# Neighbour sums of layer 0: one PSUM bank per block of rows, or two

## The chip, the cores and the metric

The kernel runs on one core of a Trainium2 chip. The metric is the device time of one execution in microseconds (us). The engines meant below are TensorE (PE, with its weight loads shown apart as PEld), VectorE (DVE), ScalarE (ACT), GpSimd (POOL) and SyncE (SP, which here only issues transfers). Each engine runs its own list of instructions strictly in the order in which the kernel issued them, and waits for others by semaphores.

## The reference, cut to what matters

Two graph layers over 4096 nodes with 512 features and a 4096 x 4096 0/1 matrix `adj`. Layer 0 is the one that is changed:

```python
Ab = A > 0
keep = Ab & (jnp.cumsum(Ab.astype(jnp.int32), axis=1) <= neibor_num)   # the first 64 neighbours
cnt = keep.sum(axis=1, keepdims=True).astype(X.dtype)
nb_sum = keep.astype(X.dtype) @ X
nb_mean = nb_sum / jnp.maximum(cnt, 1.0)
xj = jax.nn.leaky_relu(nb_mean @ W_nb.T + b_nb)
xi = jax.nn.leaky_relu(X @ W_line.T + b_line)
return xi + jnp.where(cnt > 0, xj, jnp.zeros((), X.dtype))
```

The layer's output is `x1 = layernorm(x + that)`. Layer 1 is a graph attention over all neighbours of `adj` (scores, softmax, a product with `x1 @ W`), again with a residual and a layernorm.

## The kernel before, in words

The 4096 rows are 32 blocks of 128 rows (`NB`, `P`). The kernel never forms `nb_mean @ W_nb.T`: it first computes `y = x @ W_nb.T` and then sums rows of `y`, so that the neighbour sum is `keep @ y`. `y` is kept in SBUF as two rounded parts, `y_hi` and `y_lo` (type fp32r, a float32 that PE takes in one pass), whose sum is `y` to float32's precision. The last six blocks of `y` lie in tiles named `hi` and `lo`.

Before the neighbour sums, the products with `W_nb` and `W_line` run (`seven`, L554; their matmuls are those of L512). From there on, beside the matmuls, the rows of `adj` are turned into codes in 64 steps, two for each block of rows (`NCH` is 2). One step is: SP loads a piece of `adj` (`load_adj`, L154), ACT makes flags of it (`edge`, L167), DVE scans it for the first 64 neighbours (`scan_sums` and `scan_codes`, L181 and L197: five instructions of L189, L190, L194, L201, L202), and ACT packs the outcome into bytes which POOL's queue stores to memory (`pack`, L215). After every fourth step DVE also derives the neighbour counts (`count`, L206). Thirteen of the 64 steps are done when the neighbour sums begin, and the rest are spread over them at 58/32 steps a block (`RATE`, L672): mostly two a block, sometimes one.

The neighbour sums (the loop at L725) go over 128 groups `s`, four to a block of rows `i`. A group is 8 x 128 neighbours. Its mask `kt` is made by ACT from the codes (`make_kt`, L268; the codes come back turned by a transposing transfer on SP, `load_kt`, L675). Each 128 x 128 piece of the mask is the stationary operand of two matmuls of 512 columns, one for `y_hi` and one for `y_lo`, and all 64 matmuls of a block add up in one PSUM bank, `accs[i]`. So a block is 64 matmuls and the stage 2048.

What is put in the engines' lists around this, in the order of the code, for group `s` = 4i + g:

- ACT: `make_kt(s + 2)`. It writes over the mask of group s - 1 (three buffers), so it waits for that group's matmuls. At g = 2 the activation of the block before follows, `bend0(i - 1)` (L691, instruction at L693), and then the ACT parts of a code step (`codes_late`, L248).
- SP: the transposed load for block i + 2 at g = 0, a load of `x` for block i at g = 2, and the load of `adj` for the code step two ahead.
- PE: the 16 matmuls.
- DVE: `finish(i - 1, g)` (L695), the ending of the block before. At g = 0 the sum is scaled by `rcnt` (one over the count) and the bias is added, reading the PSUM bank (L700). At g = 2 it is multiplied by `some` (count above 0), added to the rest (L706), and the layernorm's statistics follow (L118, L123, L125; the power of -1/2 is POOL's, L127). At g = 3 the layernorm is applied (L132) and the row block stored. At g = 0 of the next block two sums of products (L718) close it. `codes_step` (L254) then adds DVE's part of a code step.

So in ACT's list the activation of block i - 1, which waits for DVE's L700, stands ahead of the masks of later groups, and in DVE's list the endings and the code steps stand in one line.

PSUM has 8 banks: `ps_s` holds two (`pt`), `ps_acc` six (`acc`), which are handed out in turn. Blocks 0 and 1 take the two `pt` banks, since the `acc` banks are still in use by the stage before; block 2 and all later ones take an `acc` each. Behind the stage layer 1 takes `acc` banks from the same ring (L1217), while `finish(31, ...)` (L1152), the counts (L1159 to L1163) and their stores (L1171) stand ahead of ACT's copies of the first products (L1225).

The order within one engine is the order of the calls in the program; there is no scheduler in between.

Of the kernel before, what the change touches and what calls it, by code (L numbers as in the profile page):

```python
# [9 lines left out]
F32 = mybir.dt.float32  # L10
# [5 lines left out]
ALU = mybir.AluOpType  # L16
# [4 lines left out]
P = 128  # L21
# [11 lines left out]
def two_layer_adj_gnn(  # L33
# [16 lines left out]
    nc = tc.nc  # L50
    N, C = x.shape
    NB = N // P
    NC = C // P
# [19 lines left out]
    ps_s = ctx.enter_context(tc.tile_pool(name="ps_s", bufs=2, space=PSUM))  # L73
    ps_acc = ctx.enter_context(tc.tile_pool(name="ps_acc", bufs=6, space=PSUM))
# [12 lines left out]
    rcnt = const.tile([P, NB], F32, name="rcnt")  # L87
# [14 lines left out]
    def x1_blk(b):  # L102

        n, k = divmod(b // 2, 4)
        return x1_d[k].rearrange("(n q r) c -> n r q c", n=4, r=2)[n, b % 2]
# [4 lines left out]
    wa_rows, bias_nb = late[0:2], late[2]  # L110
# [5 lines left out]
    def ln_stats(y):  # L116
        st = stat.tile([P, nc.vector.BN_STATS_DIM], F32, name="st")
        nc.vector.bn_stats(st, y)  # L118
        return ln_rs(st)
# [10 lines left out]
    def ln_apply(y, stats):  # L130
        mv, rs = stats
        nc.vector.tensor_scalar(y, y, mv[:, 0:1], rs, ALU.subtract, ALU.mult)  # L132
# [5 lines left out]
    with ExitStack() as l0:  # L138
# [7 lines left out]
        y_hi, y_lo = ({i: t[:, i, :] for i in range(EDGE)} for t in y_most)  # L146
# [101 lines left out]
        def codes_late(n=1):  # L248

            for part, q in late_q[:n]:  # L250
                part(q)
            del late_q[:n]

        def codes_step(s):  # L254
            while done[0] < min(s, NB * NCH + 1):
                codes_late(2)
                q = done[0]
                load_adj(q + 2)
                scan(q)
                late_q.extend([(edge, q + 1), (pack_late, q - 1)])  # L260
                done[0] += 1

        KB = 8
        NS = NB // KB
        ktbs, kts, accs, owns, fin = {}, {}, {}, {}, {}
        y_again = []

        def make_kt(s):  # L268
            if s < NB * NS:
                b, g = divmod(s, NS)  # L270
                if s not in kts:
                    kts[s] = ktb_p.tile([P, KB // 2, 2, P], F32R, name="kt")
                bytes_ = ktbs[b].bitcast(U8)[:, ts(g, KB // 2), :]
                nc.scalar.activation(  # L274
                    kts[s], bytes_.rearrange("p t (i r) -> p t r i", r=2),
                    AF.Sigmoid, bias=steep[:, 1:2], scale=STEEP,
                )


        with ExitStack() as la:  # L280
# [40 lines left out]
            def early(name):  # L321
                t = adj_p.tile([P, CH], BF16, name=name).bitcast(F32)
                return t.rearrange("p (c q) -> p c q", q=C)

            raw = {}
            for name, form in (("nb", "p (c q) -> p c q"), ("line", "p (j q) -> p j q")):
                t = adj_p.tile([P, CH], I32, name="a").bitcast(F32)
# [3 lines left out]
            for k in range(2):  # L331
                t = early("left")
# [3 lines left out]
            t = early("edge")  # L336
# [336 lines left out]
        start = done[0]  # L673

        def load_kt(b):  # L675
            if b < NB:
                if packed[0] < NCH * (b + 1):
                    codes_late(2)
                assert done[0] > NCH * (b + 1)
                ktbs[b] = ktb_p.tile([P, NT, P], BF16, name="ktb")  # L680
                nc.sync.dma_start_transpose(ktbs[b], code_d[b])
# [3 lines left out]
        def place(name, bufs=2):  # L685

            if spare:
                return spare.pop(0)
            return work.tile([P, C], F32, name=name, bufs=bufs)

        def bend0(i):  # L691
            if i >= 0:
                nc.scalar.activation(fin[i], fin[i], AF.Prelu, alpha=SLOPE)  # L693

        def finish(i, g):  # L695
            if i < 0:
                return
            if g == 0:
                t = place("t")
                nc.vector.scalar_tensor_tensor(  # L700
                    t, accs.pop(i), rcnt[:, i : i + 1], bias_nb, ALU.mult, ALU.add
                )
                fin[i] = t
            elif g == 2:
                t, y = fin[i], owns.pop(i)
                nc.vector.scalar_tensor_tensor(  # L706
                    y, t, some[:, i : i + 1], y, ALU.mult, ALU.add
                )
                fin[i] = y, ln_stats(y)
            elif g == 3:  # L710
                y, stats = fin[i]
                ln_apply(y, stats)
                nc.gpsimd.dma_start(x1_blk(i), y)
            elif g == 4:
                y, _ = fin.pop(i)
                for k in range(2):
                    junk = place("junk", 1)
                    nc.vector.scalar_tensor_tensor(  # L718
                        junk, y, 1.0, wa_rows[k], ALU.mult, ALU.mult,
                        accum_out=e12[:, 1 - k, i : i + 1],  # L720
                    )
# [3 lines left out]
        for s in range(NB * NS):  # L725
            i, g = divmod(s, NS)
            if s == 2:
                for n in range(0, 4, 2):
                    hi, lo = (t[:, n : n + 2, :] for t in y_again)
                    nc.scalar.copy(hi, lo.bitcast(F32))  # L730
                    nc.vector.tensor_tensor(lo, lo.bitcast(F32), hi.bitcast(F32), ALU.subtract)
            make_kt(s + 2)
            if g == 2:
                bend0(i - 1)
            codes_late()
            if g == 0:
                load_kt(i + 2)
                if i < 2:
                    accs[i] = ps_s.tile([P, NC, P], F32, name="pt").rearrange(
                        "p k c -> p (k c)"  # L740
                    )
                else:
                    accs[i] = ps_acc.tile([P, C], F32, name="acc")
            if g == 2:
                if i < NB - 1:
                    owns[i] = place("own")
                    nc.sync.dma_start(owns[i], x_blk(i))
            if g == 3 and i < NB - 1:
                nc.gpsimd.dma_start(owns[i], own_d[i], accum_op=ALU.add)
            kt = kts.pop(s)  # L750
            turns = list(range(KB))
            if s == NS - 1:
                turns = turns[:2] + turns[6:] + turns[2:6]
            for n, k in enumerate(turns):
                j = g * KB + k
                for term in (y_hi, y_lo):
                    nc.tensor.matmul(  # L757
                        accs[i], kt[:, k // 2, k % 2, :], term[j],
                        start=(g == n == 0 and term is y_hi),
                        stop=(g == NS - 1 and n == KB - 1 and term is y_lo),  # L760
                    )
            if g == 0:
                finish(i - 2, 4)
            finish(i - 1, g)
            codes_step(start + int((s + 1) * RATE / NS))
        finish(NB - 2, 4)


# [13 lines left out]
    NS = 32  # L782
# [427 lines left out]
    for j in range(NS):  # L1210
        g, h = divmod(j, 2)
        if g < PLAIN:
# [4 lines left out]
            bank = ps_acc.tile([P, 2, HC], F32, name="acc")  # L1217
            (yrs, xvs)[g].append(bank)
            x1t = x1ts.pop(j)
            for m in range(NC):  # L1220
                nc.tensor.matmul(  # L1221
                    bank.rearrange("p h c -> p (h c)"), x1t[:, m, :], ws[:, m, :],
                    start=(m == 0), stop=(m == NC - 1),
# [23 lines left out]
    for q in range(NP * NT):  # L1247
        g, k = divmod(q, NP)
# [38 lines left out]
    p, rz = banks[NT - 1], rzs[NT - 1]  # L1287
# [64 lines left out]
```

## Time and profile before

| what | value |
|---|---|
| median of 3 runs | 1550.19 us (1549.63 to 1551.04) |
| the profiled execution, its own time | 1549.75 us |
| its span, from the first instruction to the last | 1548.0 us |
| PE busy | 1537.9 us (99% of the span) |
| DVE busy | 1265.5 us (82%) |
| ACT busy | 985.5 us (64%) |
| POOL busy | 269.5 us (17%) |
| the neighbour sums in the chain of waits | 203.85 us to 668.36 us |
| granted TensorE clock | 0.999 of full speed |

Times inside the execution are counted from the span's start. The profiled execution's time is 1.75 us longer than its span, and lies 0.44 us below the median. A row of the profile that groups instructions reads: line, engine, operation, output<-inputs (names without buffer numbers), shape, count, then busy time and mean duration. A row of the timeline reads: start, duration, engine, line, operation, output<-input, and in brackets how long the engine had been idle before and what ended that. Durations of matmuls overlap: the time that one costs is the distance from its start to the next one's. The same is true, by less, on DVE and ACT.

### The profile page before, as it was taken

How to read it: one execution, taken by the hardware profiler on the slowest of the kernel's cores; microseconds unless marked ns; L12 is line 12 of the kernel's file. 1: busy time of each engine (PE TensorE's matmuls, PEld its weight loads, DVE VectorE, ACT ScalarE, POOL GpSimd, SP SyncE). 2: the span in 40 equal slices, each digit the busy share in tenths (PEclk: the TensorE clock that was granted, in tenths of full speed). 3: DMA queues.
4: the chain of work that ended last, by engine and by line, in shares of the span. 5: the costliest groups of instructions: out<-in, count | busy, mean ns of one | idle time of the engine just before them, and what ended most of it. 6: DMA issues, size and time to landing. Idle time of an engine off the chain costs nothing.

```text
span 1548.0 us, 19196 instructions
## 1 busy us (share of the span) xinstructions
PE 1537.9 (99%) x6592; PEld 1241.4 (80%) x6592; DVE 1265.5 (82%) x2349; ACT 985.5 (64%) x1190; POOL 269.5 (17%) x428
## 2 busy tenths in 40 slices
PE   9999999999999999999999999999999999999998
PEld 5444478888888888878888888888888888888887
DVE  6888759999999999378887888888888888888864
ACT  3666678888888887427685567555675556755520
POOL 4445322212222212120001101111011110111101
PEclk9999999999999999999999999999999999999999
DMA  7965598879888887653122212222122221222201
GB/s 196 249 208 185 192 251 265 251 244 256 259 257 256 238 263 193 152 135 104 47 58 55 51 32 69 66 58 51 32 69 67 57 52 33 68 67 57 52 4 55
DMA packets 178434, 203.28 MB, mean 131 GB/s; under 512 B 102224, under 2 KB 138832, under 8 KB 170016
## 3 DMA queue, kind: packets, MB, share of 16 engines
q1 hardware_dynamic: 150080, 131.78, 30.2%
q0 software_dynamic: 26544, 68.69, 16.9%
q10 hardware_dynamic: 1712, 1.59, 0.4%
q8 instruction: 52, 0.85, 0.2%
q14 instruction: 46, 0.38, 0.1%
HBM read 142.08 MB, written 43.13 MB: 120 GB/s over the span
## 4 chain that ended last, share of the span: by engine, by line
PE 98%; DMA 1%; DVE 1%; ACT 0%; ACTq 0%; issue 0%; POOLq 0%; DVEq 0%; SPq 0%
PE acc L1094 36%; PE acc L757 28%; PE pt L1094 14%; PE acc L512 11%; PE acc L908 5%; PE pt L757 2%; PE acc L1221 1%; DMA bias_line<-in_L_gnn_b_line_dram 0%; DMA a<-in_L_gnn_W_nb_dram 0%; DMA c<-in_x_dram 0%; PE acc L373 0%; PE acc L350 0%; DVE t L406 0%; DVE hi L519 0%; DVE hi L534 0%; ACTq L292 0%
## 5 line engine op out<-in xcount | busy, mean ns | idle before, releaser
L1094 PE MATMUL acc<-bt,s 128*128 128x256 f32 x1504 | 335.7, 379 | 0.0
L1094 PEld LDWEIGHTS acc<-bt,s 128*128 128x128 f32 x1504 | 285.8, 190 | 38.9
L757 PE MATMUL acc<-y_hi,kt 128*128 128x512 f32 x780 | 303.4, 389 | 0.0
L757 PE MATMUL acc<-y_lo,kt 128*128 128x512 f32 x780 | 303.4, 389 | 0.0
L979 ACT ACTIVATE w<-nat,few 128x1024 f32<-128x1024 uint8 x128 | 137.0, 1137 | 237.8 <-DVE a L1054 237.8
L1094 PE MATMUL acc<-bt,a 128*128 128x256 f32 x1056 | 239.0, 379 | 0.0
L1094 PE MATMUL pt<-bt,a 128*128 128x256 f32 x992 | 224.5, 379 | 0.0
L1094 PEld LDWEIGHTS acc<-bt,a 128*128 128x128 f32 x1056 | 200.6, 190 | 27.3
L1094 PEld LDWEIGHTS pt<-bt,a 128*128 128x128 f32 x992 | 188.5, 190 | 25.6
L1054 DVE STREAM_TRANSPOSE a<-w 128x1024 f32<-128x1024 f32 x128 | 153.2, 1226 | 61.5 <-ACT w L1035 51.0
L274 ACT ACTIVATE kt<-ktb,few 128x1024 fp32r<-128x1024 uint8 x124 | 142.7, 1152 | 87.4 <-PE acc L757 71.7
L127 POOL TENSOR_TENSOR rs<-ve,few 128x1 f32<-128x1 f32 x64 | 46.8, 731 | 811.0 <-DVE ve L125 791.1
L757 PEld LDWEIGHTS acc<-y_lo,kt 128*128 128x128 f32 x780 | 146.5, 188 | 30.5
L757 PEld LDWEIGHTS acc<-y_hi,kt 128*128 128x128 f32 x780 | 146.3, 188 | 30.4
L972 ACT ACTIVATE w<-w,st_n 128x1024 f32<-128x1024 f32 x128 | 149.3, 1233 | 16.1 <-DVE m L989 16.1
L1035 ACT ACTIVATE w<-w,nm 128x1024 f32<-128x1024 f32 x128 | 145.5, 1138 | 11.1 <-DVE nm L1026 11.1
L989 DVE CUSTOM_DVE_ANT_0 w<-e_n,w 128x1024 f32<-128x1024 f32 x128 | 149.5, 1221 | 1.3
L171 ACT ACTIVATE edge<-a,few 128x2048 bf16<-128x2048 int32 x64 | 136.3, 2130 | 6.0 <-DMA a<-in_adj_dram 6.0
L219 ACT CAST code<-left 128x2048 uint8<-128x2048 bf16 x64 | 121.1, 1892 | 0.0
L202 DVE TENSOR_TENSOR left<-edge,left 128x2048 bf16<-128x2048 bf16 x64 | 78.4, 1225 | 2.2
L190 DVE TENSOR_TENSOR_SCAN left<-few,ends,left 128x1024 bf16<-128x1024 f32 x32 | 75.2, 2351 | 1.1
L512 PE MATMUL acc<-hi,lo 128*128 128x512 f32 x160 | 73.8, 593 | 0.4 <-ACT acc L568 0.4
(236 smaller groups left out, 2048.6 us busy)
## 6 DMA issues: line engine op xcount, KB each, us to landing
a<-in_adj_dram SPq DMA_DIRECT2D x64, 1024.0 KB, 5.7
code_d<-code POOLq DMA_DIRECT2D x64, 256.0 KB, 3.8
nat<-code_d SPq DMA_DIRECT2D x248, 64.0 KB, 2.2
w<-x_d SPq DMA_DIRECT2D x128, 64.0 KB, 2.2
own<-in_x_dram SPq DMA_DIRECT2D x31, 256.0 KB, 3.1
own<-own_d POOLq DMA_DIRECT2D x31, 256.0 KB, 4.6
x_d<-own POOLq DMA_DIRECT2D x31, 256.0 KB, 4.4
out_dram<-c POOLq DMA_DIRECT2D x30, 256.0 KB, 2.8
```

What stands on the lines that cost most here:

```text
L171: nc.scalar.activation(edge_of[s], loaded.pop(s).rearrange("p (t q) -> p q t", q=2), AF.Sigmoid, bias=steep[:, 0:1], scale=STEEP, accum_ou ...
L202: nc.vector.tensor_tensor(left, e, left, ALU.mult)
L219: nc.scalar.copy(code.bitcast(U8).rearrange("p (t q) -> p q t", q=2), seen_of.pop(s))
L274: nc.scalar.activation(kts[s], bytes_.rearrange("p t (i r) -> p t r i", r=2), AF.Sigmoid, bias=steep[:, 1:2], scale=STEEP,)
L512: nc.tensor.matmul(bank, lhs[:, k, :], rhs[:, k, :], start=start and k == 0, stop=k == 1, skip_group_check=True,)
L757: nc.tensor.matmul(accs[i], kt[:, k // 2, k % 2, :], term[j], start=(g == n == 0 and term is y_hi), stop=(g == NS - 1 and n == KB - 1 and ...
L972: nc.scalar.activation(dst, src, AF.Prelu, bias=bias, scale=scale, alpha=0.2)
L979: nc.scalar.activation(wts[b][:, i, :], nats[b, i // 2].bitcast(U8)[:, i % 2, :], AF.Relu, bias=far, scale=-FAR,)
L989: nc.vector.tensor_tensor_reduce(w_i, e2_n, w_i, 1.0, -3e38, ALU.subtract, ALU.max, m4s[b][:, i : i + 1])
L1035: nc.scalar.activation(w_i, w_i, AF.Exp, bias=nms[b][:, i : i + 1], accum_out=z4s[g][:, r, i : i + 1])
L1054: nc.vector.transpose(a[:, r].rearrange("p s (i a) -> p i s a", a=SQ), wts[2 * g + r][:, :, ts(k, 8 * SQ)].rearrange("p i (s x) -> p i s x ...
L1094: nc.tensor.matmul(banks[g][n], lhs[:, j, :], bt[:, 4 * k + j, rhs, :], start=(k == 0 and j == 0 and n == mate[0]), stop=(k == NP - 1 and ...
```

## The change

A block gets two banks instead of one. The matmuls with `y_hi` add up in the first and those with `y_lo` in the second; their order stays: `hi`, `lo`, `hi`, `lo`. The ending at g = 0 then has two DVE instructions of the same kind: the first scales the low sum and adds the bias, the second scales the high sum and adds the first one's output. Block 0 takes both `pt` banks, and all later blocks take `acc` banks in pairs, so that six banks hold three blocks where they held six. Nothing else is edited; DVE has 32 instructions more, and the lists of the other engines keep their instructions and order.

```diff
             if g == 0:
                 t = place("t")
+                of_hi, of_lo = accs.pop(i)
                 nc.vector.scalar_tensor_tensor(
-                    t, accs.pop(i), rcnt[:, i : i + 1], bias_nb, ALU.mult, ALU.add
+                    t, of_lo, rcnt[:, i : i + 1], bias_nb, ALU.mult, ALU.add
+                )
+                nc.vector.scalar_tensor_tensor(
+                    t, of_hi, rcnt[:, i : i + 1], t, ALU.mult, ALU.add
                 )
                 fin[i] = t
...
-                if i < 2:
-                    accs[i] = ps_s.tile([P, NC, P], F32, name="pt").rearrange(
-                        "p k c -> p (k c)"
-                    )
+                if i < 1:
+                    accs[i] = [
+                        ps_s.tile([P, NC, P], F32, name="pt").rearrange("p k c -> p (k c)")
+                        for _ in range(2)
+                    ]
                 else:
-                    accs[i] = ps_acc.tile([P, C], F32, name="acc")
+                    accs[i] = [ps_acc.tile([P, C], F32, name="acc") for _ in range(2)]
...
                 j = g * KB + k
-                for term in (y_hi, y_lo):
+                for bank, term in zip(accs[i], (y_hi, y_lo)):
                     nc.tensor.matmul(
-                        accs[i], kt[:, k // 2, k % 2, :], term[j],
-                        start=(g == n == 0 and term is y_hi),
-                        stop=(g == NS - 1 and n == KB - 1 and term is y_lo),
+                        bank, kt[:, k // 2, k % 2, :], term[j],
+                        start=(g == n == 0), stop=(g == NS - 1 and n == KB - 1),
                     )
```

In the changed file L700 becomes L701, the added instruction is L704, L706 becomes L710 and the matmuls' L757 becomes L762.

## The prediction

> **What bounds the kernel now.** I read the chain of waits first. PE carries 98% of it. In order of time, the stage that the change touches is one unbroken piece of PE work:
>
> ```profile
> PE 98%; DMA 1%; DVE 1%; ACT 0%; ACTq 0%; issue 0%; POOLq 0%; DVEq 0%; SPq 0%
> ...
> 203.85 29.31 PE pt L757 x128
> 233.16 435.20 PE acc L757 x1920
> 668.36 10.30 PE acc L1221 x24
> ...
> 770.46 8.63 PE acc L1094 x40
> ```
>
> (start, length, work). 435.20 us over 1920 matmuls is 226.7 ns each: 3.63 us a group of 16, 14.51 us a block. Nothing holds PE in this stage, so the question is what the other engines have to spare. The busy time by stretch, while code steps still run and after them:
>
> ```profile
> 233.00:610.00 377.00, 377.00 (x1665) 312.18 (x1664) 350.02 (x556) 315.70 (x270) 88.20 (x125) 1.00 0.86 252
> 610.00:668.36 58.36, 58.36 (x259) 48.34 (x258) 28.93 (x60) 24.23 (x23) 10.24 (x17) 1.00 0.54 128
> ```
>
> (length, then PE, PEld, DVE, ACT, POOL busy, PE's clock, DMA share, GB/s). DVE is busy 350.02 of 377 us, and the rest is hardly free time. Its waits there are:
>
> ```profile
> DVE own L132 <- POOL rs L127: 11.0, 15, 0.8
> DVE left L189 <- ACT code L219: 3.2, 3, 1.2
> DVE own L706 <- ACT t L693: 2.1, 3, 0.7
> ```
>
> The 11.0 us are a latency behind DVE's own L125: they come wherever L132 follows it directly, however late DVE is. Only 3.2 + 2.1 = 5.3 us are waits of a DVE that is early; the other 10.7 us are the steps between 556 instructions. DVE is all but full until about 618 us, where the last code step ends; behind that it is half idle.
>
> How late DVE already runs, and what stands behind it, the timelines of PE, DVE and ACT show at the start of block 21 (first matmul at 508.62):
>
> ```profile
> 508.40 0.39 PE L757 MATMUL acc<-lo,kt 128*128 128x512 f32 x1
> 508.62 0.39 PE L757 MATMUL acc<-y_hi,kt 128*128 128x512 f32 x1
> 508.85 0.39 PE L757 MATMUL acc<-y_lo,kt 128*128 128x512 f32 x1
> ```
>
> ```profile
> 516.98 0.75 DVE L700 SCALAR_TENSOR_TENSOR t<-acc,rcnt,c 128x512 f32<-128x512 f32 x1
> 518.43 0.75 DVE L706 SCALAR_TENSOR_TENSOR own<-t,e,own 128x512 f32<-128x512 f32 x1 [0.70 <-ACT t L693]
> 519.21 0.69 DVE L118 BATCH_NORM_STATS2 st<-own 128x6 f32<-128x512 f32 x1
> ```
>
> ```profile
> 501.62 1.15 ACT L274 ACTIVATE kt<-ktb,few 128x1024 fp32r<-128x1024 uint8 x1 [0.67 <-ACT code L219]
> 502.68 0.61 ACT L693 ACTIVATE t<-t 128x512 f32<-128x512 f32 x1
> 503.20 2.12 ACT L171 ACTIVATE edge<-a,few 128x2048 bf16<-128x2048 int32 x1
> 505.22 0.19 ACT L171 ACTIVATION_READ_ACCUMULATOR edge<-a,few 128x1 f32 x1
> 505.31 1.14 ACT L274 ACTIVATE kt<-ktb,few 128x1024 fp32r<-128x1024 uint8 x1
> ...
> 516.13 1.15 ACT L274 ACTIVATE kt<-ktb,few 128x1024 fp32r<-128x1024 uint8 x1 [0.67 <-ACT code L219]
> 517.76 0.63 ACT L693 ACTIVATE t<-t 128x512 f32<-128x512 f32 x1 [0.48 <-DVE t L700]
> ```
>
> The bank of block 20 was ready at 508.62, but L700 reads it at 516.98: DVE is 8.4 us late (its worst; the blocks with one code step bring it back to 3.4). ACT's L693 waited 0.48 us for it. And L693 stands between two masks: the one made at 501.62 is ready at 502.77 and used by the group that starts at 508.62, 5.85 us later, so masks are 5.85 us early; but bend, flags and the next mask fill ACT's 3.63 us of a group (501.62 to 505.31), so what L693 is late beyond 8.6 us after a block's start, the next mask is late too.
>
> **The change part by part.**
>
> *Matmuls in two banks.* Same number, order and stationary operands. Does the bank matter to PE? At 508.62 it goes to another bank (block 21 begins), and the distances are 0.22 and 0.23 us across and behind that switch, as within a block. All 31 such switches in the trace give 226 or 227 ns. Layer 1's L1094, which adds four times running into one bank, goes at 8.63 / 40 = 215.8 ns, without a slow step either. Neither a gain nor a loss: I take 0 for the 2048 matmuls, with the 226.7 - 215.8 = 10.9 ns to that row, 22.3 us in all, as the end below (a rival).
>
> [...]
>
> *Bank room and PE's new wait.* The first matmul into each bank of block i now waits for the ending of block i - 3 (before, i - 6). That ending has 29 us from its bank's completion to this wait; DVE is at most 8.4 us late now and, as below, some 15 later. 0 us. Block 1 now takes `acc` banks at 218.5 us, when the stage before is 15 us past: 0.
>
> *The added DVE instruction, 32 times.* The nearest row is L700 itself, same operation and shape, 747 ns. It reads what L701 wrote; the like pair is L706 and L118 (518.43 to 519.21), 0.78 us from start to start. Lower bound: 0.66 us, L700's distance to an instruction that does not depend on it (501.87 to 502.53). I take 0.78, as this one does depend.
>
> [...]
>
> *What of it is covered.* Endings 1 to 27 fall before the last code step: 27 x 0.78 = 21.1 us more work on DVE. The 5.3 us of waits can take some: 15.8 us remain, by which DVE falls behind PE. PE does not feel that until a mask is late. L693 may start so late that L693 (0.52 to the next start), flags (2.1) and mask (1.15) are done 5 groups, 18.13 us, after the block's start: 14.4 us. That is L701 at 14.4 - 1.56 = 12.8 us, 4.4 us above today's worst of 8.4; where no flags or packing stands between, 14.9, so 6.5. What DVE is behind at the last code step is never paid, since it then waits up to 8.3 us for L693 in blocks 29 and 30. So PE is held for 15.8 - 4.4 = 11.4 us. Ends: 21.1 - 4.4 = 16.7 (no wait shrinks); 15.8 - 6.5 = 9.3, and with the 0.66 price 27 x 0.12 less, 6.1. I take 11.4, the full price being the row's, and the flags standing there in most blocks. L700's rows have DVE 6.8 us late at block 9's ending and 7.7 at block 14's; with 0.78 an ending, less the waits so far, it passes 12.8 between the two, and PE is first held there.
>
> *What is queued behind.* SP's load of `x` waits for the store of an ended block, so a late DVE delays it and the loads of `adj` behind it on SP. ACT waited only 0.5 us for `adj`, once, near 608 us. With DVE some 8 us later against 5.85 us of early masks, 0 to 2.2 us once; I take 1.0. POOL's stores move with DVE and nobody on PE's path waits for them sooner.
>
> *Behind the stage.* `finish(31)` starts at 668.40, right after the last matmul, and ACT's copies stand at the end of its chain:
>
> ```profile
> 675.60 1.75 ACTq L1171 DMA_DIRECT2D e_d<-w  x4
> 677.70 1.59 ACT L1225 COPY bt<-acc 128x512 f32<-128x512 f32 x3 [2.50 <-DMA e_d<-w]
> ```
>
> PE's L908 comes at 678.50, just when its turn is, having waited for L1225. The chain becomes 0.78 longer: 0 to 0.8, I take 0.7. Endings 28 to 30 fall in idle time.
>
> Sum: 11.4 + 1.0 + 0.7 + 0 = 13.1 us on the profiled execution's 1549.75 (0.44 below the median, less than the runs differ): 1562.9 us.
>
> **The rivals.**
>
> *Not slower.* POOL's latency hides too: if DVE, being late, found `rs` always ready, 21.1 - 5.3 - 11.0 - 4.4 = 0.4 us would hold PE, with 0.7 behind: 1550.9. The point: added work of at most (5.3 + 11.0 + 4.4) / 27 = 0.77 us a block. Against it: that wait begins at DVE's own L125, so it does not shrink.
>
> *PE gets quicker.* If the bank did cost those 10.9 ns a matmul, the stage would not follow: until the last code step DVE sets the pace, as above, and only blocks 0, 1 and 28 to 31 gain, 6 x 64 x 10.9 ns = 4.2 us. 1549.75 + 13.1 - 4.2 = 1558.7. Against it: the 31 switches.
>
> *More than counted.* ACT's waits for DVE also delay flags and packing, which DVE then waits for, and none of the 5.3 us shrinks: 16.7 + 2.2 + 0.8 = 19.7, 1569.5 or above. For it: ACT is busy 315.70 of 377 us.
>
> [...]
>
> **How the numbers follow.** Forecast 0.78; more than counted 0.09; PE quicker 0.07; not slower 0.06. The forecast's ends are 6.1 + 0 + 0 (1555.9) and 19.7 (1569.5). Between 1557 and 1568.5 I leave out the tail of each side, the not-slower case and most of the above: 2 in 10. A change under 0.2% (3.1 us, about what a measurement of this kernel tells from none) would need the not-slower case: same 0.04, faster 0.02 (that, with PE quicker), slower 0.94.
>
> **What the profile after would show.** Matmul distance 226.7 ns within groups, with gaps at the second group of a block from about block 13 on, released by ACT's `kt`; the stage 12 to 13 us longer. L704 x32 of about 750 ns. ACT's wait for DVE's `t` from 1.2 us to tens, and its wait for PE shrunk from 46.7. DVE with hardly a wait but POOL's 11 us. L701 up to 13 to 16 us after a block's start. L908 0.7 us late. Wrong would be: another matmul distance; no gaps; or L704 overlapping L701.

## The result, and the profile after

| | before | after |
|---|---|---|
| median of 3 runs | 1550.19 us (1549.63 to 1551.04) | 1563.74 us (1563.23 to 1563.89) |
| ratio, 95% interval | | 1.0086 (1.0063 to 1.0109) |
| the profiled execution, its own time | 1549.75 us | 1563.74 us |
| its span | 1548.0 us | 1562.0 us |
| first to last matmul of the neighbour sums | 464.1 us | 476.9 us |

The changed kernel is 13.55 us slower; 13.1 was forecast on top of the profiled execution, that is 1562.9 us, in a range of 1557 to 1568.5. Between the two profiled executions the difference is 14.0 us: 12.8 in the stage, 0.9 behind it, and 0.3 ahead of it (the stage starts at 204.16 instead of 203.85), where the two kernels are the same.

The chain of waits, which PE carried almost alone before, now goes through DVE for a fifth of the span (first line, by engine). In order of time (start, length, work; from the list of its pieces) PE is still the chain at the stage's start and end, and between them stand pieces of DVE, the longest of them the scan of a code step (L190):

```profile
PE 74%; DVE 20%; issue 2%; DMA 1%; ACT 1%; POOL 1%; SPq 0%; ACTq 0%; POOLq 0%; DVEq 0%
...
218.97 50.20 PE acc L762 x222
...
481.95 2.36 DVE left L190
...
493.19 1.23 DVE left L202
...
630.38 51.09 PE acc L762 x224
```

Two waits of ACT before, until 612 us, for PE and for DVE (engine, line <- what ended the wait: us in total, times, longest):

```profile
ACT kt L274 <- PE acc L757: 46.7, 66, 2.5
...
ACT t L693 <- DVE t L700: 1.2, 3, 0.5
```

The waits of the changed kernel in the stage, of DVE, of ACT, and of PE's weight loads:

```profile
DVE own L132 <- POOL rs L127: 11.1, 15, 0.8
DVE own L710 <- ACT t L693: 2.1, 3, 0.7
...
ACT t L693 <- DVE t L704: 48.9, 17, 4.8
ACT edge L171 <- DVE left L202: 14.1, 13, 1.6
ACT kt L274 <- PE acc L762: 7.2, 12, 2.5
ACT edge L171 <- DMA a<-in_adj_dram: 6.8, 1, 6.8
...
PEld acc L762 <- ACT kt L274: 10.5, 8, 2.4
```

ACT used to wait 46.7 us for PE and 1.2 us for DVE. Now it waits 7.2 us for PE and 48.9 us for the added instruction's `t`, and PE waits for ACT's masks. DVE waits for nothing but POOL's latency and 2.1 us for ACT.

One such hold, at the second group of block 16 (the block's first matmul starts at 436.54), in the timelines of DVE, ACT and PE, in this order:

```profile
436.86 0.74 DVE L701 SCALAR_TENSOR_TENSOR t<-acc,rcnt,c 128x512 f32<-128x512 f32 x1
437.64 0.75 DVE L704 SCALAR_TENSOR_TENSOR t<-acc,rcnt,t 128x512 f32<-128x512 f32 x1
438.31 0.68 DVE L189 TENSOR_TENSOR left<-edge 128x1024 bf16<-128x1024 bf16 x1
...
438.42 0.64 ACT L693 ACTIVATE t<-t 128x512 f32<-128x512 f32 x1 [4.13 <-DVE t L704]
438.96 2.10 ACT L171 ACTIVATE edge<-a,few 128x2048 bf16<-128x2048 int32 x1
440.97 0.18 ACT L171 ACTIVATION_READ_ACCUMULATOR edge<-a,few 128x1 f32 x1
441.06 1.13 ACT L274 ACTIVATE kt<-ktb,few 128x1024 fp32r<-128x1024 uint8 x1
...
442.25 0.50 PE L762 MATMUL acc<-y_hi,kt 128*128 128x512 f32 x1 [1.92 <-ACT kt L274]
```

The ending of block 14 was due at the start of block 15. DVE began it 15.0 us later, when block 16 had already begun. ACT's activation waited 4.13 us for it, flags and mask followed, the mask was ready at 442.19, and PE went on at 442.25.

Behind the stage, PE's first L912 (L908 before):

```profile
681.29 10.46 PE L1225 MATMUL acc<-w 128*128 128x512 f32 x24
692.27 1.13 PE L912 MATMUL acc<-w,c 128*128 128x256 f32 x4 [0.52 <-ACT bt L1229]
```

It starts 11.21 us after the stage's last matmul (681.06); before, 10.53 (667.97 to 678.50), so this costs 0.7 us.

### The profile page after: what moved, and what is told of

The parts are those of the page before. It is cut to its first block, busy times and chain, and to the rows that moved or that the text cites. A ratio compares the mean times of both kernels' runs of the same rounds, so it can differ in the third digit from the quotient of the medians.

```text
span 1562.0 us, 19233 instructions
## 1 busy us (share of the span) xinstructions
PE 1543.7 (99%) x6592; PEld 1243.1 (80%) x6592; DVE 1288.6 (82%) x2381; ACT 981.8 (63%) x1190; POOL 265.5 (17%) x428
## 4 chain that ended last, share of the span: by engine, by line
PE 74%; DVE 20%; issue 2%; DMA 1%; ACT 1%; POOL 1%; SPq 0%; ACTq 0%; POOLq 0%; DVEq 0%
PE acc L1098 35%; PE pt L1098 14%; PE acc L512 11%; PE acc L762 8%; DVE left L190 6%; PE acc L912 4%; DVE left L202 2%; DVE junk L722 2%; DVE left L189 2%; DVE left L201 2%; DVE t L704 1%; DVE own L710 1%; DVE st L118 1%; DVE t L701 1%; PE pt L762 1%
## 5 line engine op out<-in xcount | busy, mean ns | idle before, releaser
L762 PE MATMUL acc<-y_hi,kt 128*128 128x512 f32 x806 | 316.4, 393 | 7.4 <-ACT kt L274 7.4
L762 PE MATMUL acc<-y_lo,kt 128*128 128x512 f32 x806 | 315.6, 392 | 0.0
L127 POOL TENSOR_TENSOR rs<-ve,few 128x1 f32<-128x1 f32 x64 | 41.7, 652 | 884.6 <-DVE ve L125 884.6
L762 PEld LDWEIGHTS acc<-y_hi,kt 128*128 128x128 f32 x806 | 152.4, 189 | 42.2 <-ACT kt L274 10.5
L762 PEld LDWEIGHTS acc<-y_lo,kt 128*128 128x128 f32 x806 | 152.4, 189 | 31.7
L171 ACT ACTIVATE edge<-a,few 128x2048 bf16<-128x2048 int32 x64 | 136.9, 2139 | 27.2 <-DVE left L202 14.1
L1039 ACT ACTIVATE w<-w,nm 128x1024 f32<-128x1024 f32 x128 | 145.5, 1137 | 11.1 <-DVE nm L1030 11.1
L202 DVE TENSOR_TENSOR left<-edge,left 128x2048 bf16<-128x2048 bf16 x64 | 78.4, 1225 | 2.2
L190 DVE TENSOR_TENSOR_SCAN left<-few,ends,left 128x1024 bf16<-128x1024 f32 x32 | 75.2, 2351 | 1.1
```

What stands on the lines that cost most here:

```text
L171: nc.scalar.activation(edge_of[s], loaded.pop(s).rearrange("p (t q) -> p q t", q=2), AF.Sigmoid, bias=steep[:, 0:1], scale=STEEP, accum_ou ...
L190: nc.vector.tensor_tensor_scan(left[:, 1], three.to_broadcast([P, CH // 2]), left[:, 0], NEIGHBORS + 3.0 if h == 0 else end, ALU.max, ALU. ...
L762: nc.tensor.matmul(bank, kt[:, k // 2, k % 2, :], term[j], start=(g == n == 0), stop=(g == NS - 1 and n == KB - 1),)
L1039: nc.scalar.activation(w_i, w_i, AF.Exp, bias=nms[b][:, i : i + 1], accum_out=z4s[g][:, r, i : i + 1])
```

## The experiments

Each loss is counted from the kernel before on the same chip, which took 1549.94 to 1550.36 us. The theory is that of the prediction: the added VectorE work overfills VectorE while code steps run; VectorE falls behind; what PE does not feel of that is a fixed room; the rest reaches PE through ACT's list. The first rival is that the second bank costs something (PE waiting for a bank, or switching); the second, that each ending pays for its own added latency.

**Two banks, one VectorE instruction.**

```diff
                 nc.vector.scalar_tensor_tensor(
-                    t, of_lo, rcnt[:, i : i + 1], bias_nb, ALU.mult, ALU.add
-                )
-                nc.vector.scalar_tensor_tensor(
-                    t, of_hi, rcnt[:, i : i + 1], t, ALU.mult, ALU.add
+                    t, of_hi, rcnt[:, i : i + 1], bias_nb, ALU.mult, ALU.add
                 )
```

> The changed kernel without the added instruction: two banks per block, but the ending reads the high sum alone, so the low part of the neighbour sum is left out of the result. Theory: within 1 us of before, 1549.5 to 1551 us, matmul distance 226.7 ns, no holds. Rival (banks): the loss stays, 1562 to 1565 us. Third reading (alternating banks make PE quicker, hidden by VectorE): faster than before by up to 22 us.

Measured: 1549.82 us, ratio 1.0001 (0.9991 to 1.0010). The chain of this run, in order of time:

```profile
203.60 14.80 PE pt L759 x64
218.41 449.71 PE acc L759 x1984
```

449.71 / 1984 is 226.7 ns a matmul, as before. Banks in pairs, their switching at every matmul and the shorter ring of banks cost PE nothing and give it nothing.

**One bank, the added instruction.**

```diff
+                one = accs.pop(i)
                 nc.vector.scalar_tensor_tensor(
-                    t, accs.pop(i), rcnt[:, i : i + 1], bias_nb, ALU.mult, ALU.add
+                    t, one, rcnt[:, i : i + 1], bias_nb, ALU.mult, ALU.add
                 )
+                nc.vector.scalar_tensor_tensor(t, one, 0.0, t, ALU.mult, ALU.add)
```

> The kernel before with one bank per block, and one more VectorE instruction per ending that reads the same bank, multiplies it by zero and adds t. Theory (the added VectorE work holds PE through ACT's list): the full loss without a second bank, 1562 to 1565 us against some 1550.2 before. Rival (the second bank costs: PE waits for banks of which six now hold three blocks, or pays for switching): no loss, 1550 to 1551 us.

Measured: 1560.71 us, ratio 1.0071 (1.0056 to 1.0086). The loss comes without any second bank; with the run above, the cause is the instruction. It is 10.8 us, 2.8 less than the change's 13.6, and the time lies 1.3 us under the range that was expected. The trace has a reason for more than half of the 2.8: with a constant in place of `rcnt` the instruction takes 692 ns instead of 751, and the step to the next is 0.61 instead of 0.67 us, 27 x 0.06 = 1.6 us. The rest is not explained.

**More and less of it.** The changed kernel with the second instruction on 64 columns (the rest of the high sum left out), on 256, and with a third instruction:

```diff
                 nc.vector.scalar_tensor_tensor(
-                    t, of_hi, rcnt[:, i : i + 1], t, ALU.mult, ALU.add
+                    t[:, :64], of_hi[:, :64], rcnt[:, i : i + 1], t[:, :64], ALU.mult, ALU.add
                 )
```

```diff
                 nc.vector.scalar_tensor_tensor(
-                    t, of_hi, rcnt[:, i : i + 1], t, ALU.mult, ALU.add
+                    t[:, :256], of_hi[:, :256], rcnt[:, i : i + 1], t[:, :256], ALU.mult, ALU.add
                 )
```

```diff
                     t, of_hi, rcnt[:, i : i + 1], t, ALU.mult, ALU.add
                 )
+                nc.vector.scalar_tensor_tensor(t, of_hi, 0.0, t, ALU.mult, ALU.add)
```

> The changed kernel with the added instruction on 64 of its 512 columns (seven eighths of the high sum are left out of the result). With the half one's rows (0.78 us from the first instruction to the second, 0.40 from the second to the next for 256 columns, against 0.66 for one alone) the price is 0.78 + 0.2 - 0.66 = 0.3 us an ending. Theory (room first): 27 x 0.3 = 8.1 us is less than the room of some 9.7 us, so no or hardly any hold: 1550 to 1552 us. Rival (proportional, 17.4 us for each us of price, from the changed kernel's 13.6 us at 0.78): 1555 us.

> The changed kernel with the added instruction on 256 of its 512 columns (half of the high sum is left out of the result). Its price is some 0.45 us (the 256-column tensor_tensor rows of the trace before take 0.42 us). Theory, with room that has to be used up first: 27 x 0.45 = 12.2, less 5.3 of VectorE's waits and 4.4 of lag that PE doesn't feel, is 2.5 us, up to 5 with fewer waits shrinking, and 0.4 behind the stage: 1553 to 1556 us. Rival (each ending pays its own instruction, no room): 13.5 x 0.45 / 0.78 = 7.8 us, 1558 us.

> The changed kernel with a third VectorE instruction per ending (the high bank times zero, added to t). Theory: the room is used up already, so all of the second 27 x 0.78 = 21.1 us is paid, and 0.8 behind the stage: some 22 us on top of the changed kernel, 1584 to 1588 us. Rival (proportional): 13.5 us on top, 1577 us.

The price is read from each run's trace: the steps from the first instruction to the last and from that to the next one, less the 0.664 us that one instruction alone needs. The last column is 27 endings times the price, less the loss: what was not paid.

| added | price an ending, us | ratio, 95% interval | loss, us | 27 x price - loss |
|---|---|---|---|---|
| nothing, two banks | 0 | 1.0001 (0.9991 to 1.0010) | -0.1 | |
| 64 columns | 0.32 | 1.0007 (0.9997 to 1.0016) | 0.9 | 7.7 |
| 256 columns | 0.52 | 1.0049 (1.0032 to 1.0066) | 7.1 | 6.9 |
| 512, one bank, constant | 0.72 | 1.0071 (1.0056 to 1.0086) | 10.8 | 8.7 |
| 512, the change | 0.786 | 1.0086 (1.0063 to 1.0109) | 13.6 | 7.7 |
| two of 512 | 1.51 | 1.0198 (1.0183 to 1.0213) | 30.8 | 10.0 |

A part of about 7 to 10 us is not paid, whatever the price, and about all beyond it is. (The losses hold the price once more, behind the stage.) The traces split that part in two. Counted from the stage's start, the last instruction of VectorE's last code step (L202) starts later than before by 5.3, 10.2, 15.6, 17.6 and 36.8 us in the last five rows; that is 3.3 to 4.0 us less than 27 times the price, about the 3.2 us that VectorE used to wait for ACT's packing. And from that L202 to the stage's last matmul it is 49.8 us before, but 43.1 to 45.0 us in these runs: 4.8 to 6.8 us by which VectorE is late and which PE never feels. With 64 columns, 27 x 0.32 = 8.6 us of added work cost 0.9 us. Proportional to the change, it would have been 0.32 x 13.6 / 0.786 = 5.5 us, and the two instructions 26 us. The run with 256 columns came out 1 us above what was expected and 1 us below the rival's 1558, so it does not decide between the two; its four times lie from 1555.4 to 1559.1 us, so that its place in the row is the least certain. The run with two instructions stayed 3.3 us below what was expected and 3.7 above the rival's 1577; of the 3.3 the cheaper constant form explains 1.6.

**VectorE relieved elsewhere.**

```diff
                         nc.vector.scalar_tensor_tensor(
-                            junk, y, 1.0, wa_rows[k], ALU.mult, ALU.mult,
+                            junk[:, :P], y[:, :P], 1.0, wa_rows[k][:, :P], ALU.mult, ALU.mult,
```

> The changed kernel with the two closing products of each block (L718 before, L722 here) on 128 of their 512 columns, so that three quarters of those dot products are left out of the result. It takes some 0.4 us off each of two instructions per ending, about the 0.78 us that the change adds, and leaves the dependent second instruction and the later activation in place. Theory (VectorE's total): no holds, 1549 to 1552 us. Rival (the activation's latency of 0.78 us a block, or the banks): 1562 to 1565 us.

Measured: 1550.12 us, ratio 1.0003 (0.9994 to 1.0012). The added instruction and its dependence are in place, and so are the two banks; only VectorE's total is back. The waits of ACT in this run:

```profile
ACT kt L274 <- PE acc L762: 69.3, 78, 2.5
...
ACT t L693 <- DVE t L704: 1.1, 3, 0.4
```

ACT waits for PE again and hardly for DVE: the later activation alone costs nothing.

**The activation behind the next mask.**

```diff
-            make_kt(s + 2)
-            if g == 2:
-                bend0(i - 1)
+            if g != 3:
+                make_kt(s + 2)
...
+            if g == 2:
+                make_kt(s + 3)
+                bend0(i - 1)
             if g == 0:
                 finish(i - 2, 4)
```

> The changed kernel with ACT's activation of an ended block (L693) one mask later in ACT's list, so that the mask that was held behind it now stands ahead of it. Reading A (the place of L693 ahead of that mask is what costs): the lag that PE doesn't feel grows by about one group, 3.6 us, and the time falls to 1559 to 1561 us. Reading B (VectorE's pace is what costs, and ACT's list only hands it on, since flags and packing still wait for VectorE and stand ahead of other masks): no gain, and with the activation 3.6 us later for VectorE's next step perhaps a loss, 1563 to 1567 us.

Measured: 1568.47 us, ratio 1.0123 (1.0108 to 1.0138): no gain, as reading B has it, but 1.5 us above its range; the loss is 18.4 us instead of 13.6. ACT's waits in it:

```profile
ACT edge L171 <- DVE left L202: 55.2, 36, 4.3
ACT kt L274 <- PE acc L761: 29.2, 21, 2.5
ACT t L693 <- DVE t L704: 12.3, 8, 3.8
```

The wait for `t` shrank from 48.9 to 12.3 us, but the wait of the flags for DVE's scan rose from 14.1 to 55.2, and they stand ahead of masks too: together 67.5 us, against 63.0. So moving L693 does not free PE; the hold passes through the flags instead. Why it is worse is shown in part: the flags wait once more, for 9.2 us, near the last code steps, and PE is held 5.9 us at one group there, against 1.0 in the changed kernel.

**Masks one group earlier.** Twice: with the third mask made ahead of the stage, and with it made first at block 2.

```diff
-                    kts[s] = ktb_p.tile([P, KB // 2, 2, P], F32R, name="kt")
+                    kts[s] = ktb_p.tile([P, KB // 2, 2, P], F32R, name="kt", bufs=4)
...
-                ktbs[b] = ktb_p.tile([P, NT, P], BF16, name="ktb")
+                ktbs[b] = ktb_p.tile([P, NT, P], BF16, name="ktb", bufs=2)
...
         make_kt(1)
+        make_kt(2)
...
-            make_kt(s + 2)
+            make_kt(s + 3)
```

and the second run against the first:

```diff
         make_kt(1)
-        make_kt(2)
...
-            make_kt(s + 3)
+            if s <= 8:
+                make_kt(s + 2)
+            if s >= 8:
+                make_kt(s + 3)
```

> The changed kernel with masks made three groups ahead instead of two (four mask buffers, and two instead of three for the turned codes). Masks are then ready 9.4 us early instead of 5.8. Theory (a lag that PE doesn't feel is used up once, then VectorE's pace rules): the room grows once by a group, 3.6 us, and the time falls by about that to 1559.5 to 1561 us, still above before. Rival 1 (each ending costs by itself, no room): unchanged, 1563 to 1564.5 us. Rival 2 (the masks' lead is the whole cause): back to 1550 to 1552 us.

> As the run with masks three groups ahead, but the third mask is made first at block 2, so that the stage starts as in the changed kernel (the run before held PE for some 1.5 us and let VectorE start 3 us later there). Theory (room that is used up once, here one group of 3.6 us larger): 1559 to 1561 us, some 3.5 us less than the changed kernel. Rival 1 (no such room): 1563 to 1564.5 us. Rival 2 (the masks' lead is the whole cause): 1550 to 1552 us.

Measured: 1562.13 us, ratio 1.0079 (1.0062 to 1.0096), and 1559.81 us, ratio 1.0063 (1.0048 to 1.0078). The first is 1.1 us above the range that was expected and says little: the mask made ahead held PE by some 1.5 us at the stage's start and began the first ending 3.4 us later. The second lies in its range: the loss is 9.5 us, 4.1 less than the change's 13.6; a group is 3.63 us. The room grew by one group and was used up once; the rest of the loss stayed. It is no version to keep, since the kernel before is still 9.5 us quicker. None of the runs suggests one that beats it: two banks alone give PE nothing.

## Why the prediction was right

- *Matmuls in two banks, 0.* Right: 226.7 ns with one VectorE instruction, and the loss is there with one bank. The 31 switches between blocks in the trace before had told it. The rival's 10.9 ns a matmul never was a price of the bank: L1094, the row that it is taken from, has 256 columns of plain float32, and L757 has 512 of fp32r; in the trace before, a matmul of the program is two records there, 215.8 ns each, and one here, 226.7 ns.
- *Price 0.78 us.* Measured 0.782 + 0.668 - 0.664 = 0.786 us.
- *Held in the stage, 11.4 + 1.0 us.* The stage is 12.8 us longer. The way is as foretold: DVE's lag in the stage, ACT's L693, a late mask, PE. The parts of the sum fit less well than the total, and that they meet at 12.8 is in part luck. Of VectorE's 5.3 us of waits, the 3.2 for ACT's packing went, but the 2.1 for L693 stayed, so 2.1 us were missing from the sum. Against that, SP's 1.0 should not have been added: VectorE waited for nothing but POOL and L693 up to 630 us and reached the end of its code steps 17.6 us later than before, counted from the stage's start, and less the 4.8 us that are never paid this is the whole 12.8, SP's hold within it. That hold itself came at the size taken: ACT waited once for `adj`, 6.8 us, and PE was held about 1.1 us behind it. But on SP that load stood behind a transposed load, which had waited 11.0 us for a store of codes, and not behind a load of `x`.
- *What is never paid.* At the last endings before the code steps end VectorE was 8.2 us late against 3.4 before: 4.8 us unpaid, for a predicted 4.4. L202's distance to the stage's end says the same, 49.8 less 45.0.
- *First hold.* Forecast for a lag that passes 12.8 us between the endings of blocks 9 and 14. A trace of it (0.07 us) shows in block 15, the first real one (2.08 us) in block 16. VectorE's lag was 12.7 us at block 13's ending and 15.0 at block 14's, so it passed 12.8 at the late edge of what was forecast. Five of the holds are at the second group of a block, as foreseen, two at the third.
- *Behind the stage, 0.7 us.* Measured 0.7 at the first L912 and 0.1 more by the next wait, 0.8.
- *The clock.* Missed: the sum has no term for it, and the clock halved twice (below). 16 matmuls are thereby 0.2 us longer each, 3.2 of the 12.8 us. It did not add to the sum: VectorE never waited for PE from 233 to 630 us, and its 17.6 us less 4.8 are the 12.8 already. The hold and the slow matmuls of block 16 took 2.1 and 1.6 us from VectorE's lag, and block 17 had no hold.
- *The rivals.* "Not slower" needed POOL's latency to shrink; it is 11.1 us, as before (11.0). "More than counted" needed none of VectorE's waits to shrink; the 3.2 us did, and the loss stayed 6 us short of its 19.7. "PE quicker" fell with the matmul distance.

## What to carry to other kernels

When the bounding engine shows no gap, add up the busy time, the fixed latencies and the issue steps of the engine behind it in that same stage: 350 us busy of 377 here left 5.3 us of waits, of which 3.2 could be used, not 27. In these runs an instruction added to such an engine cost about its full price times its count, less a room that is used up once: those waits, and the lag that the lead of the bounding engine's input hides (one group of 3.63 us more lead gave 4.1 us). And an engine's list that mixes work for the bounding engine with waits for the full one hands the full one's pace on; moving one such wait behind a mask did not help, since the next one took its place.

## What the runs showed of the hardware

The clock of PE halved after short holds. The changed kernel's profile, in stretches around the hold of block 16 (length, then PE, PEld, DVE, ACT, POOL busy with counts, PE's clock, DMA share, GB/s):

```profile
440.00:443.37 3.37, 1.45 (x7) 0.95 (x6) 3.30 (x5) 3.37 (x4) 0.00 (x0) 1.00 0.33 63
443.37:446.79 3.42, 3.42 (x10) 2.65 (x9) 2.57 (x6) 3.42 (x3) 1.49 (x3) 0.50 1.03 348
446.79:450.00 3.21, 3.21 (x16) 2.66 (x15) 3.14 (x4) 3.21 (x5) 1.28 (x2) 1.00 0.96 201
```

After a stretch in which PE was busy 1.45 of 3.37 us, its clock is 0.50 for 3.41 us, and matmuls start 427 ns apart instead of 226.7. This came twice in the stage, from 443.37 and from 610.63, each time 1.1 us after the end of a hold: of 2.08 us at block 16, and of 2.09 us until 609.56 (distance between matmul starts beyond 226.7 ns). After the stage's other holds, of at most 1.38 us, the clock stayed at 1.00. In the run with one bank, two stretches with PE busy 1.48 of 3.42 and 1.51 of 3.40 us were each followed by one of 3.4 us at 0.50. These few holds give no rule.

The added VectorE instruction took 692 ns with a constant 0.0 as its scalar (one bank) and 751 ns with a column of `rcnt` (the change), with the same shapes and the same kinds of operands otherwise.
